# The last two row tiles of a graph layer: matrix products spread between transposes, row counts gathered, column sums copied by two engines

## The chip, the core and the metric

The kernel runs on one core of one Trainium2 chip. The metric is the device time of one execution in microseconds, the median of several runs. A core has five engines with instruction streams of their own: TensorE (matrix products and transposes, results in the accumulator memory PSUM), VectorE, ScalarE and GpSimd (element-wise work), and SyncE, which here only issues DMA transfers. Each works through its stream in order, and semaphores hold an instruction until what it needs is there.

## What is computed

Four graph layers run over 2708 nodes with 128 features each, on one dense 2708 x 2708 matrix `adj` in which few entries are not zero. Each layer normalises and rectifies its input, applies a graph operation, and adds the result to its input. The change concerns layer 0 and the start of layer 1.

```python
# layer 0
h = jnp.maximum(_layernorm(x, axis=-1), 0.0)
x = x + _L0_gnn_ref(h, adj)      # (adj.T @ h) / adj.sum(axis=0)[:, None]
# layer 1
h = jnp.maximum(_layernorm(x, axis=-1), 0.0)
x = x + _L1_gnn_ref(h, adj, ...) # messages gelu(s[i] + d[j] + b), weighted by adj[i, j], summed over j
# layer 2: aggregate adj @ h, then a gated recurrent unit
# layer 3: two heads of masked attention
```

Layer 1 needs one message for each entry of `adj` that is not zero. So layer 0, which reads all of `adj` anyway, also lists those entries.

## The kernel before

Rows are cut into 22 row tiles of 128 (the last has 20 rows) and the row tiles into six groups: five of four tiles and a last one of two (tiles 20 and 21, 148 rows in all). Columns are cut in two ways: for the products into six chunks (five of 512 columns and one of 148), for the lists into 22 blocks of 124.

Layer 0 does four things with each row tile:

- `load_row_tile` brings it from memory; two sets of four tiles are held at a time.
- `aggregate_rows(n, ci)` multiplies the normalised features of tile `n` with chunk `ci` of the tile, on TensorE, and adds to accumulator `ci`. Six accumulators of one PSUM bank each are filled over all 22 tiles: a tile has six such products.
- `turn_blocks(gi, j)`, called a turn below, transposes column block `j` of all tiles of group `gi` on TensorE into one of two PSUM buffers. ScalarE copies it out as `aT` and sums the columns by the way (`sums`), and a DMA writes it to memory for layers 2 and 3. A turn of the last group holds only two transposes and 148 columns.
- `list_row_tile` finds the entries: for each of the 22 blocks VectorE takes the eight largest values of every row (`val`) and their columns (`col`). `sign_sums` has ScalarE count a row's entries with one long pass over the tile and then copy the diagonal block `dg`, which GpSimd prepares.

The instructions are in an order written out by hand (`tc.manual_schedule()`). The loop over groups emits, for each of the 22 turns `j`, the turn, then the products that are due, and at turns 1, 3, 6, 8 and so on the lists and sign sums. For groups of four, products are spread over the turns, `len(steps) * (j + 1) // NT` of them by turn `j`. The first group is different: its products come ahead of all its turns (`ahead`). So it is with the last group too.

After the loop ScalarE copies the six accumulators from PSUM to `sumT` in on-chip memory, and VectorE turns the column sums into reciprocals (`deg`, `inv`). Layer 1 then takes over the same PSUM banks and much of the same on-chip memory.

Layer 1 begins with a start-up list of steps. `spread_sums(g)` transposes a group of `sumT` on TensorE. `enter(g)` scales it by `inv` and adds it to `x` on VectorE, with the moments for the next normalisation; `rows(g)` normalises on ScalarE; `turn_rows(g)` transposes back. `count_rows(t)` counts, for row tile `t`, how many of the eight values of each block and row are above zero, with two VectorE instructions, into `rows_n[:, t, :]`. `rank(t)` sums these counts over the rows above with one product on TensorE, which VectorE copies out (`ends`). `select_rows`, `finish_rows`, `fetch` and `place` build from that the matrices that pick source and destination rows; `destinations` and `split_destinations` make the messages' second half. From row tile 4 on, the counts are made inside the periods of layer 1 that follow, one per row tile. Steps of one engine follow each other in the order of this list.

Of the kernel before, what the change touches and what calls it, by code (L numbers as in the profile page):

```python
# [21 lines left out]
BF16 = mybir.dt.bfloat16  # L22
AF = mybir.ActivationFunctionType
ALU = mybir.AluOpType
AX = mybir.AxisListType
# [5 lines left out]
P = 128  # L31
N = 2708
D = 128
NT = (N + P - 1) // P
# [10 lines left out]
NB = (N + JB - 1) // JB  # L45
S = 8
# [14 lines left out]
def listed_layers(ctx: ExitStack, tc: tile.TileContext, x, adj, w, out, flag):  # L61
    nc = tc.nc
# [100 lines left out]
    keep = lists.enter_context(tc.tile_pool(name="keep", bufs=1))  # L163
# [21 lines left out]
    ends4 = keep.tile([P, NB, R], BF16, name="ends4")  # L185
    rows_n = keep.tile([P, NT, NB], BF16, name="rows_n")
    ends = keep.tile([P, NT, NB], BF16, name="ends")
    later = keep.tile([P, NB, E], BF16, name="later")
    nc.gpsimd.memset(later, 0.0)
    xb = [keep.tile([P, NB, C], BF16, name=f"xb{q}") for q in range(2)]  # L190
# [13 lines left out]
    with tc.tile_pool(name="l0c", bufs=1) as fix:  # L204
# [29 lines left out]
        def normal_rows(g):  # L234
            t, k = GROUPS[g]
            scale_rows(tiles_of(h, t, k), tiles_of(xs, t, k), rstd[:, t - 4 :], shifts[:, t - 4 :], AF.Relu)

        with (
            tc.tile_pool(name="l0", bufs=2) as rows,
            tc.tile_pool(name="l0k", bufs=2) as pool,  # L240
            tc.tile_pool(name="l0t", bufs=8) as turned,
            tc.tile_pool(name="l0p", bufs=1, space=PSUM) as acc,
        ):
            accs = [acc.tile([P, CH], F32, name=f"acc{c}") for c in range(len(CHUNKS))]
            sets, marks = {}, {}

            def load_row_tile(n):
                gi, q, m = n // 4, n % 4, size(n)
                if q == 0:
                    sets[gi] = rows.tile([P, 4, N], F32, name="a")  # L250
                if m < P:
                    nc.gpsimd.memset(sets[gi][:, q, :], 0.0)
                nc.sync.dma_start(sets[gi][0:m, q, :], adj[n * P : n * P + m, :])

            def list_row_tile(n):

                m = size(n)
                a = sets[n // 4][:, n % 4, :]
                d0 = n * P
                b0 = d0 // JB  # L260
                b1 = (d0 + m - 1) // JB
                c0, c1 = b0 * JB, min((b1 + 1) * JB, N)
                near = pool.tile([P, 3 * JB], F32, name="near")
                nc.gpsimd.tensor_copy(near[:, 0 : c1 - c0], a[:, c0:c1])
                nc.gpsimd.tensor_tensor(
                    near[:, d0 - c0 : d0 - c0 + m], a[:, d0 : d0 + m], offdiag[:, 0:m], ALU.mult
                )
                marks[n] = pool.tile([P, P], F32, name="dg")
                nc.gpsimd.tensor_tensor(marks[n][:, 0:m], a[:, d0 : d0 + m], ident[:, 0:m], ALU.mult)

                def block(b):
                    if b0 <= b <= b1:
                        return near[:, b * JB - c0 : b * JB - c0 + width(b)]
                    return a[:, b * JB : b * JB + width(b)]

                blocks = [b for b in range(NB) if not b0 <= b <= b1] + list(range(b0, b1 + 1))
                if n >= LATER:
                    late_blocks.extend((n, b) for b in range(NB) if not b0 <= b <= b1)
                    blocks = range(b0, b1 + 1)
                for k in range(0, NB, 2):  # L280
                    for b in blocks[k : k + 2]:
                        nc.vector.max(val[:, n, b, :], block(b))  # L282
                    for b in blocks[k : k + 2]:
                        nc.vector.max_index(col[:, n, b, :], val[:, n, b, :], block(b))  # L284

            def sign_sums(n):
                m = size(n)
                sign = pool.tile([P, N], BF16, name="sign")
                nc.scalar.activation(sign, sets[n // 4][:, n % 4, :], AF.Sign, accum_out=total[:, n : n + 1])
                dg = marks.pop(n)[:, 0:m]  # L290
                nc.scalar.activation(dg, dg, AF.Copy, accum_out=own[:, n : n + 1])

            def aggregate_rows(n, ci):
                c, cw = CHUNKS[ci]
                m = size(n)
                nc.tensor.matmul(  # L296
                    accs[ci][:, 0:cw], h[0:m, n, :], sets[n // 4][0:m, n % 4, c : c + cw],
                    start=(n == 0), stop=(n == NT - 1),
                )

            def turn_blocks(gi, j):
                g0, gk = GROUPS[gi]
                i0, iw = span(g0, gk)
                k = size(j)
                p = bank("p_T")
                for q in range(gk):
                    m = size(g0 + q)
                    nc.tensor.transpose(  # L308
                        p[0:k, q * P : q * P + m], sets[gi][0:m, q, j * P : j * P + k], ident[0:m, 0:m]
                    )  # L310
                aT = turned.tile([P, CH], F32, name="aT")
                nc.scalar.activation(aT[0:k, 0:iw], p[0:k, 0:iw], AF.Copy, accum_out=sums[0:k, j, gi : gi + 1])  # L312
                nc.sync.dma_start(adjT[0:k, j, i0 : i0 + iw], aT[0:k, 0:iw])

            with tc.manual_schedule():
                for n in range(8):
                    load_row_tile(n)
                    if n == 1:
                        load_rest()
                for gi, (g0, gk) in enumerate(GROUPS):  # L320
                    steps = [(n, ci) for n in range(g0, g0 + gk) for ci in range(len(CHUNKS))]
                    ahead = gi == 0 or gk < 4
                    for n in range(g0, g0 + gk):
                        if ahead:
                            for ci in range(len(CHUNKS)):
                                aggregate_rows(n, ci)
                        if n < 2:
                            list_row_tile(n)
                            sign_sums(n)
                            (sum_rows, sum_squares)[n](pool)  # L330
                    done = 0
                    for j in range(NT):
                        turn_blocks(gi, j)
                        now = len(steps) * (j + 1) // NT
                        for step in steps[done:now]:
                            if not ahead:
                                aggregate_rows(*step)
                        done = now
                        n = g0 + j // 5
                        if j % 5 == 1 and j // 5 < gk and n > 1:  # L340
                            list_row_tile(n)
                        if j % 5 == 3 and j // 5 < gk and n > 1:
                            sign_sums(n)
                        if gi > 0 and j % 4 == 3 and j < 16 and g0 + 4 + j // 4 < NT:
                            load_row_tile(g0 + 4 + j // 4)
                        if j == NT - 2 and gi + 1 < len(GROUPS):
                            normal_rows(gi + 1)
                for ci, (c, cw) in enumerate(CHUNKS):
                    nc.scalar.copy(sumT[:, c : c + cw], accs[ci][:, 0:cw])


        deg = fix.tile([P, 3, NT], F32, name="deg")
# [36 lines left out]
    with (  # L389
# [429 lines left out]

        with tc.manual_schedule():  # L820
            for step, n in (
                (spread_sums, 0), (count_rows, 0), (spread_sums, 1), (rank, 0), (enter, 0),
                (select_rows, 0), (describe, 0), (enter, 1), (spread_sums, 2), (rows, 0), (turn_rows, 0),
                (count_rows, 1), (rows, 1), (count_rows, 2), (count_rows, 3), (destinations, 0), (turn_rows, 1),
                (finish_rows, 0), (fetch_both, 0), (rank, 1), (enter, 2), (spread_sums, 3), (select_rows, 1),
                (split_destinations, 0), (destinations, 1), (describe, 1), (rows, 2), (turn_rows, 2),
                (place, 0), (pass_on, 0), (sources, 0), (enter, 3), (spread_sums, 4), (split_destinations, 1),
                (destinations, 2), (rows, 3), (turn_rows, 3), (finish_rows, 1), (fetch_both, 1), (enter, 4),
                (spread_sums, 5), (columns, 0), (place, 1), (split_destinations, 2), (destinations, 3), (rows, 4),
                (turn_rows, 4), (enter, 5), (rank, 2), (select_rows, 2), (rows, 5), (turn_rows, 5), (describe, 2),  # L830
                (split_destinations, 3), (put_values, 0), (destinations, 4), (put_rest, 0), (finish_rows, 2),
            ):
                step(n)
# [865 lines left out]
```

## Time and profile before

| | |
|---|---|
| time, median of 3 runs | 1076.99 us (1075.41 to 1079.09) |
| profiled execution, span | 1076.2 us |
| TensorE matmul busy | 950.2 us (88%) |
| VectorE busy | 824.4 us (77%) |
| ScalarE busy | 516.5 us (48%) |
| mean granted TensorE clock | 0.934 of full speed |

Busy time is the time in which an engine worked on an instruction. The idle time ahead of an instruction is put down to the engine or transfer that released it last, after the arrow: `[3.16 <-ACT hT L349]` is 3.16 us of idle time that ended when ScalarE's instruction of line 349, which writes `hT`, was done. (`hT` is the trace's name for the memory of `sumT`, which layer 1 uses again.) In the trace PE is TensorE's products and transposes, PEld its weight loads, DVE VectorE, ACT ScalarE, POOL GpSimd, SP SyncE; L and a number is a line of the kernel. The granted clock is the share of full speed at which TensorE was let run. The chain of work that ended last says little here: it reaches back only to 1069.26 us. So the timelines of single engines have to be read.

### The profile page before, as it was taken

The numbers are of one execution on the slowest core, as the hardware profiler recorded it, in microseconds if no ns is written. First come the engines' busy times: TensorE is split into PE (matmuls) and PEld (weight loads), VectorE is DVE, ScalarE is ACT, GpSimd is POOL, SyncE is SP. The second block draws the span as 40 slices with busy tenths as digits, with TensorE's granted clock in tenths as the row PEclk, the third lists the DMA queues.
The fourth block names the chain that finished last, engine by engine and source line by source line (L and its number), as shares of the span: only waits on it lengthen the run. The fifth ranks groups of instructions, "written<-read, shape, count | busy, mean of one in ns | idle before, by whom it ended". The sixth has DMA issues, their size and how long they took to land. (4 is left out here: it accounts for less than half of the span.)

```text
span 1076.2 us, 21996 instructions
## 1 busy us (share of the span) xinstructions
PE 950.2 (88%) x7950; PEld 756.6 (70%) x7950; DVE 824.4 (77%) x2856; ACT 516.5 (48%) x1431; POOL 398.0 (37%) x476
## 2 busy tenths in 40 slices
PE   5798889854699999999999979999978999999993
PEld 2454455433599999899998934444578999999762
DVE  7999999658577888887878265666578977997673
ACT  7777778444666566666576522333321200320142
POOL 3311112013686556666765253434410300440132
PEclk9999999755799999999999979999989999999996
DMA  9888897221133333223222065666300000000000
GB/s 367 312 308 291 311 344 257 57 72 55 54 124 103 118 115 112 83 85 108 85 89 75 29 215 199 206 215 211 106 21 26 7 3 1 6 16 1 1 16 14
DMA packets 60625, 129.67 MB, mean 120 GB/s; under 512 B 11160, under 2 KB 23828, under 8 KB 57798
## 3 DMA queue, kind: packets, MB, share of 16 engines
q1 hardware_dynamic: 58690, 125.38, 33.7%
q10 hardware_dynamic: 1816, 2.80, 0.8%
q8 instruction: 64, 1.05, 0.4%
q14 instruction: 55, 0.45, 0.1%
HBM read 81.55 MB, written 30.87 MB: 104 GB/s over the span
## 5 line engine op out<-in xcount | busy, mean ns | idle before, releaser
L949 PE MATMUL att<-hv,wt 128*128 128x129 f32 (+2 forms) x1936 | 243.8, 283 | 8.8 <-DVE wt L917 8.8
L949 PEld LDWEIGHTS att<-hv,wt 128*128 128x128 f32 (+2 forms) x1936 | 224.7, 192 | 25.7 <-DVE wt L917 10.2
L917 DVE SCALAR_TENSOR_TENSOR wt<-row,lift,mask 128x1024 f32<-128x1024 f32 (+5 forms) x176 | 160.2, 939 | 35.1 <-PE att L949 35.1
L530 POOL TENSOR_SCALAR put<-mine,value 128x128 f32<-128x128 bf16 x176 | 149.6, 866 | 70.3 <-DVE mine L427 68.0
L606 PE MATMUL p_m<-s,sel 128*128 128x128 bf16 x1452 | 161.6, 220 | 5.4 <-ACT g L618 5.4
L610 PE MATMUL p_m<-d,cols 124*128 124x128 bf16 (+1 forms) x1452 | 161.8, 220 | 1.4 <-DVE cols L560 1.3
L121 POOL TENSOR_TENSOR n_r<-n_r,minus_half 128x4 f32<-128x4 f32 (+1 forms) x31 | 46.1, 1486 | 292.4 <-DVE n_r L120 286.8
L631 PE MATMUL agg<-put,g 128*128 128x128 f32 (+1 forms) x968 | 135.9, 281 | 0.0
L296 PE MATMUL acc<-a,hs 128*128 128x512 f32 (+2 forms) x264 | 119.8, 563 | 11.1 <-ACT hs L137 11.1
L308 PEld LDWEIGHTS p_T<-ident,a 128*128 128x128 f32 x484 | 61.3, 147 | 85.7 <-issue 38.4
L631 PEld LDWEIGHTS agg<-put,g 128*128 128x128 f32 x968 | 118.2, 192 | 0.0
L1088 PE MATMUL p_agg<-a,hs 128*128 128x512 f32 (+2 forms) x264 | 109.4, 557 | 7.5 <-DMA a<-adjT 7.5
L606 PEld LDWEIGHTS <-sel 128*128 128x128 bf16 x1452 | 104.3, 98 | 10.8 <-issue 7.0
L308 PE MATMUL p_T<-ident,a 128*128 128x128 f32 x484 | 84.3, 295 | 30.9 <-ACT aT L312 23.5
L284 DVE FIND_INDEX8 col<-val,a 128x8 uint16<-128x124 f32 (+1 forms) x400 | 109.2, 290 | 0.0
L610 PEld LDWEIGHTS <-cols 124*128 124x128 bf16 (+1 forms) x1452 | 102.6, 98 | 1.9 <-DVE cols L560 1.9
L618 ACT ACTIVATE g<-p_m 128x512 f32<-128x512 f32 x132 | 73.0, 553 | 63.5 <-PE p_m L610 63.5
L538 ACT ACTIVATE put<-mine,value 128x128 f32<-128x128 bf16 x308 | 100.5, 391 | 0.0
L312 ACT ACTIVATE aT<-p_T 128x512 f32<-128x512 f32 (+2 forms) x132 | 71.1, 541 | 52.8 <-ACT aT L312 27.6
L282 DVE MAX8 val<-a 128x8 f32<-128x124 f32 (+1 forms) x400 | 94.2, 282 | 2.1 <-DMA a<-in_adj 2.1
L1088 PEld LDWEIGHTS p_agg<-a,hs 128*128 128x128 f32 (+1 forms) x264 | 47.6, 194 | 55.9 <-issue 54.3
L296 PEld LDWEIGHTS acc<-a,hs 128*128 128x128 f32 (+1 forms) x264 | 44.6, 199 | 31.2 <-issue 19.9
(249 smaller groups left out, 1423.7 us busy)
## 6 DMA issues: line engine op xcount, KB each, us to landing
a<-in_adj SPq DMA_DIRECT2D x21, 1354.0 KB
adjT<-aT SPq DMA_DIRECT2D x105, 256.0 KB
a<-adjT SPq DMA_DIRECT2D x20, 1280.0 KB
spread<-passed SPq DMA_DIRECT2D x22, 704.0 KB
later<-sel SPq DMA_DIRECT2D x22, 616.0 KB
row<-own_d ACTq DMA_DIRECT2D x10, 256.0 KB
later<-sel SPq DMA_DIRECT2D x22, 82.5 KB
adjT<-aT SPq DMA_DIRECT2D x21, 74.0 KB
```

The lines of the kernel that those rows point to most:

```text
L282: nc.vector.max(val[:, n, b, :], block(b))
L284: nc.vector.max_index(col[:, n, b, :], val[:, n, b, :], block(b))
L296: nc.tensor.matmul(accs[ci][:, 0:cw], h[0:m, n, :], sets[n // 4][0:m, n % 4, c : c + cw], start=(n == 0), stop=(n == NT - 1),)
L308: nc.tensor.transpose(p[0:k, q * P : q * P + m], sets[gi][0:m, q, j * P : j * P + k], ident[0:m, 0:m])
L530: nc.gpsimd.tensor_scalar(st["put", 0][:, b, :], st["mine"][:, b, :], st["value"][:, b : b + 1], None, ALU.mult)
L538: nc.scalar.activation(st["put", 1][:, b - HP, :], st["mine"][:, b, :], AF.Identity, scale=st["value"][:, b : b + 1])
L606: nc.tensor.matmul(p[:, b - b0, :], st["sel"][:, b, :], s3[:, q, t % 2, :], start=(q == 0), stop=False)
L610: nc.tensor.matmul(p[:, b - b0, :], st["cols"][0:kb, b, :], d3[0:kb, b, q, :], start=False, stop=(q == 2))
L631: nc.tensor.matmul(agg, g[:, b - 4 * k, :], put, start=(b == 0), stop=False)
L917: nc.vector.scalar_tensor_tensor(wt[0:kj, :], row[0:kj, k, c : c + n], lift[0:kj, j, k : k + 1], mask[0:kj, j, c : c + n], op0=ALU.max, op ...
L949: nc.tensor.matmul(banks[s // 3][0:m, s % 3, :], wt[0:kj, q * P : q * P + m], hv[0:kj, j, k, :], start=(v < 2 and s // 3 not in touched), ...
L1088: nc.tensor.matmul(pa[:, 0:n], h[0:k, j, :], a[0:k, j - j0, 0:n], start=(j == 0), stop=(j == NT - 1))
```

## The change

Three edits, all at the end of layer 0 and the start of layer 1.

First, the last group is no longer one whose products come ahead. One product follows each of its first twelve turns. Second, the counts of row tiles 0 to 3 are no longer four steps of layer 1's start-up. They are made at the end of layer 0 by two instructions over all four tiles at once, into a buffer of their own, `some4`, that is kept beside `rows_n`. Third, the copies of accumulators 0, 2 and 4 go to VectorE, and those of 1, 3 and 5 stay on ScalarE.

The aim of the first is to give ScalarE turns to copy while TensorE multiplies; of the second, to take small instructions out of the start-up; of the third, to have two engines share the copies that layer 1 waits for.

```diff
+    some4 = keep.tile([P, 4, NB, S], BF16, name="some4")
...
-                    ahead = gi == 0 or gk < 4
+                    ahead = gi == 0
...
-                        now = len(steps) * (j + 1) // NT
+                        now = len(steps) * (j + 1) // NT if gk == 4 else min(len(steps), j + 1)
...
+                nc.vector.tensor_scalar(some4, val[:, 0:4, :, :], 0.0, None, ALU.is_gt)
+                with nc.allow_low_precision("counts up to 8"):
+                    nc.vector.reduce_sum(rows_n[:, 0:4, :], some4, AX.X)
                 for ci, (c, cw) in enumerate(CHUNKS):
-                    nc.scalar.copy(sumT[:, c : c + cw], accs[ci][:, 0:cw])
+                    copy = nc.vector.tensor_copy if ci % 2 == 0 else nc.scalar.copy
+                    copy(sumT[:, c : c + cw], accs[ci][:, 0:cw])
...
-                (spread_sums, 0), (count_rows, 0), (spread_sums, 1), (rank, 0), (enter, 0),
+                (spread_sums, 0), (spread_sums, 1), (rank, 0), (enter, 0),
                 (select_rows, 0), (describe, 0), (enter, 1), (spread_sums, 2), (rows, 0), (turn_rows, 0),
-                (count_rows, 1), (rows, 1), (count_rows, 2), (count_rows, 3), (destinations, 0), (turn_rows, 1),
+                (rows, 1), (destinations, 0), (turn_rows, 1),
```

## The prediction

> **What bounds the kernel now.** I read the page first for the shares (TensorE busy 88%, VectorE 77%, ScalarE 48%). These are averages over four layers; the change touches only the last group of layer 0 and the hand-over to layer 1. I went from the page to the busy time by stretches, then to the timeline of each engine between 186 and 250 us. Columns of the stretches: length, busy time and count of TensorE matmuls, its weight loads, VectorE, ScalarE and GpSimd, then granted TensorE clock, DMA share, GB/s.
>
> ```profile
> 175.00:200.00 25.00, 23.22 (x90) 12.50 (x91) 25.00 (x171) 14.16 (x36) 3.65 (x9) 0.99 0.42 143
> 200.00:225.00 25.00, 17.12 (x57) 9.93 (x55) 7.45 (x49) 15.80 (x58) 0.68 (x3) 0.50 0.27 80
> ```
>
> Up to about 205 us VectorE is never idle (row lists) and sets the pace of layer 0. After that no engine is full: from 200 to 225 us VectorE works 7.45 us of 25. The timelines tell who waits for whom (start, length, engine, line, operation, count, idle time before it and its releaser):
>
> ```profile
> 190.03 11.37 PE L296 MATMUL acc<-a,hs 128*128 128x512 f32 x28
> 201.33 3.83 PE L308 MATMUL p_T<-ident,a 128*128 128x128 f32 x12
> ...
> 212.81 6.78 PE L308 MATMUL p_T<-ident,a 128*128 128x128 f32 x22 [2.18 <-ACT aT L312]
> 222.75 1.97 PE L758 MATMUL p_m<-ident,hT 128*128 128x128 f32 x8 [3.16 <-ACT hT L349]
> ```
>
> ```profile
> 202.11 0.29 ACT L312 ACTIVATE aT<-p_T 128x148 f32<-128x148 f32 x1 [10.68 <-issue]
> ...
> 209.74 2.45 ACT L289 ACTIVATE sign<-a 128x2708 bf16<-128x2708 f32 x1
> ...
> 220.06 2.64 ACT L349 COPY hT<-acc 128x512 f32<-128x512 f32 x6
> ```
>
> ```profile
> 219.80 0.25 DVE L421 TENSOR_SCALAR some<-val 128x176 bf16<-128x176 f32 x1 [14.32 <-ACT aT L312]
> ```
>
> The tail is a chain: TensorE does all 12 products of the two last row tiles (to 201.4 us) while ScalarE sits idle 10.68 us; then 22 turns go from TensorE to ScalarE and back, with two sign sums between them, to 220.15 us; then ScalarE copies six accumulators, and only then does TensorE start layer 1 at 222.75 us, 3.16 us idle. VectorE has nothing for 14.3 us.
>
> [...] the granted clock falls at 199.64, rises at 240.60 and falls at 244.01, and 40.96 is 12 times 3.41. The fall comes with TensorE full, in a window holding only products of the last tile, which has 20 rows:
>
> ```profile
> 192.81:196.23 3.42, 3.42 (x10) 1.00 0.00 0
> 196.23:199.64 3.41, 3.41 (x9) 1.00 0.00 0
> 199.64:203.05 3.41, 3.41 (x10) 0.50 0.01 2
> ```
>
> (TensorE alone: length, busy time and count, clock, DMA share, GB/s.) [...]
>
> **The change part by part.**
>
> *Products between the transposes.* Warm, the 512-column products of the last tiles follow each other every 0.86 us (two records 0.43 apart), the 148-column one takes about 0.25; at half clock double. A turn is two transposes: 0.30 us warm (four took 0.60), 0.63 cold. ScalarE needs 0.48 per turn (0.29 + 0.19) and 3.1 per row tile for sign sum and diagonal (2.45 + 0.19 + 0.30 + 0.19). Two PSUM buffers let TensorE run two turns ahead.
> New timeline from 191.2 us, where TensorE ends group 4: turns 0 to 3, each with a product, 1.16 apart; ScalarE ends turn 3 at 195.5. The sign sum of tile 20 keeps it to 198.6, so TensorE stalls before turn 6, from 197.5 to 199.0. Turns 6 to 8 with products of tile 21 follow warm to 202.5. The sign sum of tile 21 starts at 202.2 and the diagonal copy behind it needs GpSimd's tile: that product waits on VectorE's list and ends at 204.92 in before; VectorE's order there is unchanged. So ScalarE resumes at about 205.4. By then I expect the clock to have fallen (203.05, as the 20-row products again hold little work), so product 21/4 ends at 206.3 and turn 11 near 206.9. A short product (0.5), then ten cold turns at 0.63 and the last ScalarE pass end at about 214.3, against 220.15: **5.85 us**.
> Bounds: warm to the end, 13 turns at 0.48 after 205.4 end at 211.9 (8.2 us gained). Cold already from 199.64, the products take 1.72 each, tile 21's sign sum ends at 207.1 and the last turn at 217.2 (3.0 gained).
>
> *Copies on two engines.* Six copies took 2.64 us. ScalarE keeps two long and the short one: 2.64 - 3 x 0.47 = 1.2 us after the last turn. VectorE's three, about 0.68 each (a 128x387 evacuation took 0.555 and a 128x129 one 0.292, so 1.02 ns per element and 125 elements more), wait only for products that end by 207 and lie in its idle stretch. Gain **1.4 us**, since TensorE's first work of layer 1 waits for all copies to release the banks.
>
> *Counts in one go.* Two instructions over four tiles, scaled from 0.24 and 0.34 us for one tile: 0.8 to 1.4 each, in VectorE's idle 14 us after 205.4, ahead of the copies. Together with the three copies VectorE is done near 210, before the column sums that need the last turn. Eight small instructions leave the start of layer 1: four pairs of about 0.57. The first pair lay beside ScalarE's copies. The others lie before a wait that VectorE has anyway:
>
> ```profile
> 236.27 1.61 DVE L477 TENSOR_TENSOR sel<-sel,later 128x2816 bf16<-128x2816 bf16 x1
> ...
> 240.49 0.18 DVE L456 CAST ends<-p_r 128x22 bf16<-128x22 f32 x1 [2.61 <-PE p_r L455]
> ```
>
> There TensorE is held by its own order (transposes, ScalarE's copy, destination products, second transposes), so the 1.7 us removed only lengthen the 2.61 us wait. I count **0** (at most 1.7).
>
> *New waits.* VectorE's copy of the first accumulator waits for product 21/0; behind it queue the other copies and the column-sum chain, which cannot start before the last ScalarE pass anyway. TensorE's turns of the last group now wait behind products: the loss is in the timeline above.
>
> Sum: 5.85 + 1.4 = 7.2 us. Everything after the start of layer 1 is tied to it, not to absolute times; I see no transfer or earlier work that would pin a later stage. 1077.0 - 7.2 is **1069.8 us**, which I call 1070.0.
>
> **The rivals.**
> A, the clock falls early: [...] For it: windows with 0.76 and 1.14 us of busy time dropped the clock at 46.0 and 90.4 us. Against it: one with 1.77 us kept it, and I expect about 1.9. Gain 3.0 + 1.4: 1072.6.
> B, the tail shortens but layer 1's start gives it back, because VectorE or a weight load is late: the message weights are issued at 221.74 us only after the column-sum chain, which keeps its distance of 1.6 us from the last turn while the copies shrink by 1.4. Against it: their first user comes at 225.38, and destinations at 236.83. Only the copies would be left: 1075.6.
> C, slower: all the tail runs cold. 10 x 1.72 + 2 x 0.5 + 22 x 0.63 from 191.2 give a last turn near 223.4, 3.2 later; less 1.4, plus one more cold window when layer 1's dense products start (1.7 us): 1080.5. For it: 41 us after 199.64 are at half clock. Against it: the window before holds full 128-row products.
>
> **How the numbers follow.** Forecast 0.66 (gain 4.6 to 9.6), A 0.18, B 0.11, C 0.05. The bound warm case reaches 8.2 + 1.4, so 1067.4, the cold one 1072.6; with runs of before spread 1075.41 to 1079.09 I take about 1.5 us more at each end: 1066.0 to 1074.0, leaving out B, C and little else. Faster by over 0.3% (3.2 us) is the forecast and most of A, 0.84; within 0.3% is B and a part of A, 0.11; slower 0.05.
>
> **What would show it.** In the changed profile: ScalarE's idle gap of 10.68 us gone; the last turn at 212 to 217 us; three ScalarE copies of about 1.2 us together after it and three VectorE copies before it; layer 1's first transposes 6 to 9 us earlier; the wait before the second rank longer than 2.61 us. It would be wrong if the last turn comes after 218 us, if the distance from layer 1's first transposes to the dense products (284.97 us, where the clock rises) grows, or if the clock falls before 199 us.

## The result and the profile after

The changed kernel takes 1071.51 us (median of 4 runs, 1071.37 to 1073.93) where the kernel before, run beside it, takes 1077.44 (1075.41 to 1079.09). The ratio is 0.9951 with a 95% interval of 0.9929 to 0.9974, so the change saves about 5.9 us. A later series gave 0.9953 (0.9938 to 0.9969). The two profiled executions differ by 6.6 us (1076.2 and 1069.6).

The same stretches as before, of the kernel after (length, then TensorE, weight loads, VectorE, ScalarE, GpSimd, clock, DMA share, GB/s):

```profile
175.00:200.00 25.00, 23.23 (x97) 12.21 (x95) 25.00 (x171) 18.71 (x52) 3.37 (x8) 1.00 0.48 158
200.00:225.00 25.00, 17.79 (x53) 8.79 (x52) 15.89 (x71) 9.76 (x38) 3.71 (x6) 0.56 0.25 73
```

ScalarE's work moved forward: 18.71 us in the first stretch where it had 14.16. VectorE works 15.89 us in the second, where it had 7.45: its copies and counts lie in the idle stretch, and layer 1's start has moved in.

TensorE's timeline of the kernel after (start, length, line, operation, count, idle time before it and its releaser):

```profile
189.37 1.28 PE L297 MATMUL acc<-a,hs 128*128 128x512 f32 x4
190.49 0.44 PE L309 MATMUL p_T<-ident,a 128*128 128x128 f32 x2
190.85 1.12 PE L297 MATMUL acc<-a,hs 128*128 128x512 f32 x2
191.82 0.44 PE L309 MATMUL p_T<-ident,a 128*128 128x128 f32 x2
...
198.44 0.49 PE L309 MATMUL p_T<-ident,a 128*128 128x128 f32 x2 [0.42 <-ACT aT L313]
...
204.72 0.70 PE L309 MATMUL p_T<-ident,a 128*128 128x128 f32 x2
205.25 2.05 PE L297 MATMUL acc<-a,hs 20*128 20x512 f32 x2
207.23 0.70 PE L309 MATMUL p_T<-ident,a 128*128 128x128 f32 x2
207.77 0.84 PE L297 MATMUL acc<-a,hs 20*128 20x148 f32 x2
208.53 6.16 PE L309 MATMUL p_T<-ident,a 128*128 128x128 f32 x20
216.42 1.97 PE L764 MATMUL p_m<-ident,hT 128*128 128x128 f32 x8 [1.73 <-ACT hT L355]
```

Products and turns alternate from 190.49 us, and TensorE waits only 0.42 us for ScalarE's first sign sum. The starts tell the price: at full clock (warm, 1.00 granted) a turn and its product take 1.33 us (190.49 to 191.82), at half clock (cold, 0.50) 2.51 (204.72 to 207.23), of which the product takes 1.98. The wait before layer 1's first transposes fell from 3.16 to 1.73 us.

ScalarE and VectorE of the kernel after:

```profile
214.89 0.27 ACT L313 ACTIVATE aT<-p_T 20x148 f32<-20x148 f32 x1
215.06 0.18 ACT L313 ACTIVATION_READ_ACCUMULATOR aT<-p_T 20x1 f32 x1
215.16 1.21 ACT L355 COPY hT<-acc 128x512 f32<-128x512 f32 x3
```

```profile
205.03 0.51 DVE L350 TENSOR_SCALAR some<-val 128x704 bf16<-128x704 f32 x1
205.57 0.89 DVE L352 TENSOR_REDUCE rows_n<-some 128x88 bf16<-128x704 bf16 x1
206.38 1.88 DVE L355 COPY hT<-acc 128x512 f32<-128x512 f32 x3
215.28 0.29 DVE L360 TENSOR_REDUCE deg<-sums 128x22 f32<-128x132 f32 x1 [7.03 <-ACT aT L313]
```

Three ScalarE copies of 1.21 us follow the last turn; VectorE's counts and copies are done by 208.26 us and it then sits idle 7.03 us.

The clock (TensorE alone: length, busy time and count, clock, DMA share, GB/s):

```profile
199.67:203.08 3.41, 3.41 (x12) 1.00 0.25 73
203.08:206.49 3.41, 3.41 (x6) 0.50 0.17 45
```

It falls at about 203.08 us, after a stretch of 20-row products and turns in which TensorE was full (3.41 us of 3.41).

To compare runs I use four marks of each profiled execution: A, the start of group 4's last products (190.03 before, 189.37 after); T, the end of ScalarE's last turn; S, layer 1's first transposes; G, layer 1's first product of the gather (`agg<-put,g`). Times from A take out the up to 3 us by which executions differ on the way to the last group (A lies between 187.17 and 190.03 us). The table's distances are worked out from the timelines; "fall" is the clock's fall counted from A.

| kernel | fall | A to T | T to S | S to G | A to G | end |
|---|---|---|---|---|---|---|
| before | 9.6 | 30.12 | 2.60 | 66.8 | 99.5 | 1076.2 |
| after | 13.7 | 25.87 | 1.18 | 66.6 | 93.7 | 1069.6 |
| after, again | 12.3 | 27.07 | 1.17 | 66.7 | 94.9 | 1069.1 |
| products only | 12.6 | 26.69 | 2.61 | 66.7 | 96.1 | 1070.0 |
| copies only | 9.8 | 29.91 | 1.18 | 66.7 | 97.7 | 1071.0 |
| counts only | 8.2 | 31.51 | 2.60 | 66.8 | 100.9 | 1075.5 |
| all copies on VectorE | 12.5 | 29.79 | (-7.20) | 73.0 | 95.6 | 1069.4 |
| five copies on VectorE | 12.8 | 26.52 | 0.22 | 66.6 | 93.3 | 1067.1 |
| last tile over 128 rows | 20.5 | 24.66 | 1.18 | 66.6 | 92.5 | 1067.7 |
| alternating tiles | 16.9 | 26.11 | 1.17 | 66.6 | 93.9 | 1065.1 |
| five copies, 128 rows | 20.2 | 25.09 | 0.22 | 66.6 | 91.9 | 1067.1 |
| the same, late diagonal | 21.2 | 23.95 | 0.23 | 66.6 | 90.8 | 1064.0 |

In the last row the clock had also fallen 0.7 us after A and risen again at 4.1.

From G on, executions differ by up to 4 us in layers 2 and 3 (from layer 3's first product to the end 287.6 to 291.9 us), with no order by edit. I did not study this; it is why single spans are not compared here.

### The profile page after: what moved, and what is told of

Same layout as the page of the kernel before. It is cut to its first block, busy times and chain, and to the rows that moved or that the text cites. A ratio compares the mean times of both kernels' runs of the same rounds, so it can differ in the third digit from the quotient of the medians.

```text
span 1069.6 us, 21992 instructions
## 1 busy us (share of the span) xinstructions
PE 950.0 (89%) x7950; PEld 754.1 (71%) x7950; DVE 824.4 (77%) x2853; ACT 515.4 (48%) x1428; POOL 398.7 (37%) x476
## 5 line engine op out<-in xcount | busy, mean ns | idle before, releaser
L297 PE MATMUL acc<-a,hs 128*128 128x512 f32 (+2 forms) x264 | 124.4, 574 | 10.8 <-ACT hs L137 10.8
L297 PEld LDWEIGHTS acc<-a,hs 128*128 128x128 f32 (+1 forms) x264 | 44.7, 202 | 25.9 <-issue 14.8
```

The source lines that it names most:

```text
L297: nc.tensor.matmul(accs[ci][:, 0:cw], h[0:m, n, :], sets[n // 4][0:m, n % 4, c : c + cw], start=(n == 0), stop=(n == NT - 1),)
```

## The experiments

### Each part alone

The first leaves counts and copies as before:

```diff
-                    ahead = gi == 0 or gk < 4
+                    ahead = gi == 0
...
-                        now = len(steps) * (j + 1) // NT
+                        now = len(steps) * (j + 1) // NT if gk == 4 else min(len(steps), j + 1)
```

> Only the products of the last two row tiles are put between the turns; counts and copies stay as in the kernel before. Theory (the tail from the last group's start to the last turn shrinks by 4.2 us, the copies give 1.4 apart from it, the counts nothing): time 1073.2, the last ScalarE pass of the turns about 25.9 us after the start of group 4's last products (30.1 before), then 2.6 us until layer 1's first transposes as before. Rival (the counts or copies carry most of the gain): time above 1075.5, and less than 2 us shorter from group 4's last products to the last turn.

Measured: 1074.02 us, ratio 0.9970 (0.9952 to 0.9987). A to T is 26.69 us, T to S 2.61. The first rival falls: the products carry most of the gain. The 25.9 expected was missed by 0.8, and the clock had fallen 1.1 us earlier than in the kernel after.

The second shares the copies only:

```diff
-                    nc.scalar.copy(sumT[:, c : c + cw], accs[ci][:, 0:cw])
+                    copy = nc.vector.tensor_copy if ci % 2 == 0 else nc.scalar.copy
+                    copy(sumT[:, c : c + cw], accs[ci][:, 0:cw])
```

> Only the six copies are shared by VectorE and ScalarE. Theory: layer 1's first transposes start 1.2 us instead of 2.6 us after the last turn, the last turn stays 30.1 us after group 4's last products, time 1076.0. Rival (the copies lie beside other work, since the column-sum chain and weight loads hold layer 1 anyway): the first transposes come earlier but the distance from them to the end grows by the same 1.4 us, time 1077.4.

Measured: 1075.59 us, ratio 0.9992 (0.9978 to 1.0006), too near to no change for the time alone to decide. The trace decides: T to S is 1.18 us where it was 2.60, and S to G is 66.7, no longer than before (66.8). So 1.4 us is gained and not given back by G.

The third gathers the counts only:

```diff
+                nc.vector.tensor_scalar(some4, val[:, 0:4, :, :], 0.0, None, ALU.is_gt)
+                with nc.allow_low_precision("counts up to 8"):
+                    nc.vector.reduce_sum(rows_n[:, 0:4, :], some4, AX.X)
...
-                (spread_sums, 0), (count_rows, 0), (spread_sums, 1), (rank, 0), (enter, 0),
+                (spread_sums, 0), (spread_sums, 1), (rank, 0), (enter, 0),
...
-                (count_rows, 1), (rows, 1), (count_rows, 2), (count_rows, 3), (destinations, 0), (turn_rows, 1),
+                (rows, 1), (destinations, 0), (turn_rows, 1),
```

> Only the counts of row tiles 0 to 3 are gathered at the end of layer 0. Theory: nothing on the path, time 1077.4 within noise, the wait before VectorE's second rank copy grows from 2.6 to about 3.9 us. Rival (small VectorE instructions at layer 1's start are on the path): 1.0 to 1.7 us less between layer 1's first transposes and the end.

Measured: 1077.08 us, ratio 1.0000 (0.9987 to 1.0013). S to G is 66.8 us, as before. VectorE's timeline of this run shows where the removed time went:

```profile
233.74 1.62 DVE L481 TENSOR_TENSOR sel<-sel,later 128x2816 bf16<-128x2816 bf16 x1
239.23 0.18 DVE L460 CAST ends<-p_r 128x22 bf16<-128x22 f32 x1 [3.87 <-PE p_r L459]
```

The wait for TensorE's second rank is 3.87 us, where it was 2.61. The counts bought nothing in time. A to T is 1.4 us longer here than before; that is the clock, which fell 8.2 us after A, 1.4 us earlier than before, in the middle of the products (12.75 us of busy time, 11.37 before).

Added up, the medians of the three runs give 3.4 us (2.7 and 1.1, less 0.4), where the whole change gave 5.9 and later 4.7. Each of the three is uncertain by 1.4 to 1.9 us, so the times alone do not show that the parts add up, and no run joins just two of them. The traces do add up to G: the products alone take 96.1 us from A to G, less 1.4 for the copies 94.7, and the changed kernel takes 93.7 and 94.9.

### Are ScalarE's copies still on the path?

```diff
-                    copy = nc.vector.tensor_copy if ci % 2 == 0 else nc.scalar.copy
+                    copy = nc.vector.tensor_copy
```

> The changed kernel with all six copies on VectorE. Theory (ScalarE's three copies after the last turn still sit on the path, VectorE is idle 7 us before the column sums): VectorE's six copies take 3.8 us and end near 211, layer 1's first transposes start 0.1 to 0.2 us after the last turn, 1.0 to 1.1 us gained on the changed kernel: 1070.4. Rival (the column-sum chain of 1.3 us that starts after the last turn takes the place of the copies): the first transposes come 1.1 us earlier, but VectorE's first use of the reciprocals does not, time as the changed kernel, 1071.5.

Measured: 1071.66 us, ratio 0.9948 (0.9930 to 0.9966). It is as fast as the changed kernel, as the rival said, but for neither reason. The order between the two hand-written parts is not fixed: with no ScalarE copy behind the last turn, layer 1's transposes were placed among the turns. TensorE's timeline of this run:

```profile
210.10 0.69 PE L764 MATMUL p_m<-ident,hT 128*128 128x128 f32 x2 [1.13 <-DVE hT L355]
210.58 0.64 PE L309 MATMUL p_T<-ident,a 128*128 128x128 f32 x2
211.16 0.47 PE L764 MATMUL p_m<-ident,hT 128*128 128x128 f32 x1
211.43 0.64 PE L309 MATMUL p_T<-ident,a 128*128 128x128 f32 x2
```

TensorE waits 1.13 us for the last copy in the middle of the turns and then does other work between them. A to T grows to 29.79 us, and everything after needs the reciprocals that come only after T. So I kept the short copy on ScalarE, which holds the order:

```diff
-                    copy = nc.vector.tensor_copy if ci % 2 == 0 else nc.scalar.copy
+                    copy = nc.vector.tensor_copy if ci < 5 else nc.scalar.copy
```

> The changed kernel with five copies on VectorE and only the short one (148 columns) on ScalarE, so that TensorE's first transposes of layer 1 still stand after the last turn in its order. Theory: layer 1's first transposes start 0.3 us after the last turn (1.18 in the changed kernel), and 0.9 us less from group 4's last products to the end; time about 1070.6. Rival (the column-sum chain of 1.3 us after the last turn takes over): the first transposes start at 0.3 us, but the distance from them to the end grows by about as much, time as the changed kernel.

Measured: 1068.99 us, ratio 0.9932 (0.9908 to 0.9955). T to S is 0.22 us and S to G 66.6, so 1.0 us is gained from T to G and the column-sum chain does not take over. The theory holds, by the trace. By the medians this version is 2.5 us below the changed kernel, which was timed in another series; the intervals of the two ratios overlap, and the 1.5 us more are not explained.

### Why does the clock fall?

One run does the last tile's products over all 128 rows (the rows beyond 20 are zeros):

```diff
-                    accs[ci][:, 0:cw], h[0:m, n, :], sets[n // 4][0:m, n % 4, c : c + cw],
+                    accs[ci][:, 0:cw], h[:, n, :], sets[n // 4][:, n % 4, c : c + cw],
```

> The changed kernel with the products of the last tile over all 128 rows (the 108 rows beyond the 20 are zeros in both operands). Theory (the clock falls because 20-row products count as little work): the granted clock stays full until at least 207 us, products of the last tile stay at 0.97 us, the last turn ends 1.5 to 3.5 us earlier relative to group 4's last products (22.4 to 24.4 us after them, 25.9 in the changed kernel), time 1069. Rival (the clock falls for the idle gaps at the sign sums, or the zeros count as no work): the clock falls 12 to 15 us after group 4's last products as in the changed kernel, and nothing moves.

Measured: 1069.52 us, ratio 0.9929 (0.9907 to 0.9951). The last tile's 512-column products stand in the same place and take about as long (1.12 us of busy time each, 1.10 in the kernel after, both warm), and the clock holds longer (TensorE alone, columns as above):

```profile
197.82:201.23 3.41, 3.41 (x12) 1.00 0.27 77
201.23:204.65 3.42, 2.30 (x6) 1.00 0.07 19
204.65:208.06 3.41, 2.56 (x13) 1.00 0.29 85
208.06:211.47 3.41, 3.41 (x11) 0.50 0.43 126
```

It falls at 208.06 us, 20.5 after A, when the products are over and only turns are left. The stretch from 201.23 has more idle time (1.12 us) than the one after which the clock fell in the changed kernel (none), and the clock stays at 1.00 behind it. So in these two runs the fall goes with the rows of the products (20 rows, 13.7 us after A; 128 rows, 20.5), not with TensorE's idle time. The other runs agree: all three with 128 rows keep the clock to 20.2 to 21.2 us after A (one of them after a short early fall, see below), the five that spread 20-row products one tile after the other lose it at 12.3 to 13.7. (There are falls after idle time too: in the kernel after the clock also fell at 158.72 us, after a stretch in which TensorE was busy 1.38 us of 3.41.) A to T is 24.66 us, 1.2 less than after. That is less than the 1.5 to 3.5 expected, because another wait now ends last. ScalarE's and TensorE's timelines of this run:

```profile
204.67 0.22 ACT L292 ACTIVATE dg<-dg 128x20 f32<-128x20 f32 x1 [1.94 <-POOL dg L270]
```

```profile
205.30 0.49 PE L309 MATMUL p_T<-ident,a 128*128 128x128 f32 x2 [1.78 <-ACT aT L313]
```

ScalarE stands at tile 21's diagonal copy for 1.94 us, and TensorE behind it for 1.78. In the second profile of the changed kernel ScalarE stood there too, for 2.25 us, but TensorE, at half clock, was still busy with products and did not wait. With the clock held it is done with them earlier and has to wait.

The other run lets the two tiles alternate:

```diff
+                    if gk < 4:
+                        steps.sort(key=lambda s: s[1])
```

> The changed kernel with the products of tiles 20 and 21 taking turns (20/0, 21/0, 20/1, 21/1 ...). Theory (20-row products count as little work): [...] the clock holds about 3.4 us longer, to 206 us or later, and the last turn ends 0.5 to 2 us earlier; time 1070.5. Rival: the clock falls where it did, nothing moves.

Measured: 1067.83 us, ratio 0.9921 (0.9893 to 0.9949). The clock holds to 204.22 us, 16.9 after A, 3.2 longer than after, as the theory said. But A to T is 26.11 us, no shorter: ScalarE waits 2.17 us at the same diagonal copy, and TensorE 2.57 behind it. So this fall came after idle time as well: TensorE was busy 2.00 us in the stretch ahead of it. The low time of this run arises mostly in layer 3 (287.6 us to the end, 288.9 to 291.9 in the others), where no edit reaches, so I don't credit it to the order of the tiles.

### Both, and the wait behind them

Five copies on VectorE together with 128 rows:

> Both: five copies on VectorE and the last tile's products over 128 rows. If both theories hold, the last turn ends 22.4 to 24.4 us after group 4's last products, layer 1's first transposes 0.3 us later, time about 1068. If only the first holds, 1070.6.

Measured: 1068.30 us, ratio 0.9934 (0.9909 to 0.9958). T to S is 0.22 us as expected, A to T 25.09, which misses the 22.4 to 24.4 for the wait just named (2.33 us of ScalarE here). The last run moves that diagonal copy:

```diff
-                dg = marks.pop(n)[:, 0:m]
+                if n < NT - 1:
+                    own_sums(n)
+
+            def own_sums(n):
+                dg = marks.pop(n)[:, 0 : size(n)]
                 nc.scalar.activation(dg, dg, AF.Copy, accum_out=own[:, n : n + 1])
...
+                        if gi == len(GROUPS) - 1 and j == 16:
+                            own_sums(NT - 1)
```

> Five copies on VectorE, the last tile's products over 128 rows, and ScalarE's diagonal copy of tile 21 moved from behind its sign sum (turn 8) to behind turn 16, with its own wait on GpSimd. Theory (with the clock held, the next bound of the tail is ScalarE waiting at that copy for GpSimd's block, which waits for VectorE's list: 1.94 us idle until 204.67 in the run before): that wait is gone, the last turn ends 1.5 to 2.5 us earlier, 22.5 to 23.5 us after group 4's last products, and layer 1's first transposes 0.2 us later; time about 1066.5. Rival (TensorE or VectorE ends the tail anyway): the last turn stays at 24.7 to 25.1 us, time about 1068.3.

Measured: 1066.55 us, ratio to before 0.9916 (0.9894 to 0.9939); the changed kernel in the same series took 1071.62. The wait is gone; ScalarE's timeline of this run:

```profile
203.79 0.28 ACT L317 ACTIVATE aT<-p_T 128x148 f32<-128x148 f32 x1
...
208.09 0.21 ACT L296 ACTIVATE dg<-dg 128x20 f32<-128x20 f32 x1
```

It takes up the turns at 203.79 us, straight after the sign sum. A to T is 23.95 us, outside the 22.5 to 23.5 expected. The clock had fallen at 187.88 us, 0.7 after A and before the last group's first turn (188.66), and rose at 191.30, so the group's first product was cold: 2.08 us of busy time, against 1.12 for the later, warm ones. ScalarE's first sign sum starts 7.50 us after A, 5.91 in the kernel after; by this estimate the cold start cost 1.6 us of the tail. This version beats the changed kernel: 5.1 us by the medians of this series, 4.1 us up to G (90.8 against 94.9 from A).

The changed kernel itself, run beside it:

> The changed kernel once more, beside the next one. Every theory: about 1071.5. From its trace: if the clock falls in another place relative to the last group, the distance from group 4's last products to the last turn moves with it (25.9 us when it fell 13.7 us after them, 26.5 to 26.7 when it fell 12.6 to 12.8 us after them); from layer 1's first transposes to its first gather product 66.7 us as in all runs.

Measured: 1071.62 us, ratio 0.9953 (0.9938 to 0.9969). The clock fell 12.3 us after A and A to T was 27.07 us: earlier fall, longer tail, as expected.

## Why the prediction was right

- **What bounds the tail.** Right. With the products spread alone, A to T fell by 3.4 us (30.12 to 26.69), and ScalarE's idle gap of 10.68 us is gone.
- **Products between the transposes, 5.85 us.** Right in kind, too large: 4.25 in the profiled pair (30.12 less 25.87). The term that was off is the price of a turn and its product: I took 1.16 us warm and 2.35 cold (0.63 + 1.72), and they take 1.33 and 2.51; the short cold product I took at 0.5 takes 0.76. Up to the first sign sum this cost nothing: TensorE comes to it later, but then waits 0.42 us instead of 1.5 and goes on only 0.1 us later than predicted (all relative to A). After that the third product of tile 21 ends 0.7 us later, the fifth 1.6, the last turn 1.6.
- **Why the pair was dearer.** That the kinds take turns is not the reason. In group 4 of the kernel before they do so already, with four transposes to a product:

```profile
184.85 0.60 PE L308 MATMUL p_T<-ident,a 128*128 128x128 f32 x4
185.29 1.02 PE L296 MATMUL acc<-a,hs 128*128 128x512 f32 x2
186.15 0.60 PE L308 MATMUL p_T<-ident,a 128*128 128x128 f32 x4
```

By the starts this pair takes 0.44 + 0.86 = 1.30 us. With two of the four transposes it should take less, but in the kernel after it takes 0.36 + 0.97. What is new is the second transpose of each turn, which is over 20 rows. In group 4 a transpose starts 0.11 us after the one ahead of it. In the kernel after the 20-row one starts 0.20 us after the 128-row one, the product 0.16 after that, and the product's second half 0.53 later instead of 0.43. My estimate from these distances is that the time goes where the number of rows changes; no run tests this.
- **The clock.** Predicted to fall at 203.05 us, 13.0 after A. It fell at 203.08, which is 13.7 after A, and in the second profile at 199.55, 12.3 after A. That the first agrees to 0.03 us is luck, since A moves by up to 3 us between executions. The reason given, 20-row products, is the one that the 128-row run supports (fall 20.5 us after A). Rival A, a fall one stretch earlier for the wait at the first sign sum, did not come: that wait is 0.42 us. But where the fall lands moves the tail: T comes 25.87 us after A in the first profile and 27.07 in the second, so the 4.25 above holds for one pair of profiles only. Three profiles without spread products have 29.91 to 31.51, four with them (the changed kernel twice, products only, five copies) 25.87 to 27.07.
- **GpSimd's block at the diagonal copy.** Predicted to hold ScalarE until 205.4, 15.4 us after A. In the kernel after ScalarE takes up turns at 204.81, also 15.4 after A, but its sign sum had just ended, so GpSimd did not hold it. In the second profile it did. TensorE was at half clock both times and did not wait for it; with the clock held it did.
- **Copies, 1.4 us.** T to S fell from 2.60 to 1.18: 1.42. Alone the same. The copies of the two engines never run at the same time here: VectorE's are done at 208.26 us, ScalarE's begin at 215.16. Elsewhere both engines read PSUM at the same time: in the run with the late diagonal VectorE's five copies (206.42 to 209.49 us) run beside ScalarE's copies of turns. They take 3.07 us, as long as five of 0.68 us started 0.60 apart would at the pace of the kernel after (4 x 0.60 + 0.68 = 3.08), and a turn's copy takes 0.29 us in both.
- **Counts, 0.** S to G is 66.8 before and 66.8 with the counts alone. Two instructions took 0.51 and 0.89 us in idle time, and the wait before the second rank is 3.87 us in the kernel after, longer than 2.61, as predicted.
- **Rivals B and C.** S to G did not grow, so nothing was given back; the tail did not run cold from its start.
- **The warm bound.** Its sum is slightly off: 13 turns of 0.48 us from 205.4 end at 211.6, not 211.9.

Sum: 4.25 + 1.42 is 5.7 of the 7.2 predicted, near the 5.9 of the medians. The remaining 0.9 between the two profiles is an arrival at A 0.66 us earlier and 0.27 after S, neither of which I put down to the change.

## What to carry to other kernels

When two engines hand work to and fro and one has independent work in a block ahead of that, spread it between the hand-overs: it fills waits that both engines have (ScalarE's idle gap of 10.68 us is gone here), up to the point where one of them is full (here TensorE from 199.67 us, 3.41 us of 3.41). Price such a mix from a stretch in which the same shapes follow each other in the same order: no warm stretch of the kernel before had a 20-row transpose next to a product, and the prices read there were too low. Small instructions are worth removing only where no wait follows them on the same engine; read that wait first (here it grew from 2.61 to 3.87 us). And when a bound falls, look for the next instruction that stands in order behind something late: here moving one diagonal copy shortened A to T by 1.1 us (25.09 to 23.95), and the counts gave nothing.

## What the runs showed of the hardware

- Products over 20 rows took about as long as over 128 (1.10 and 1.12 us of busy time, warm), but the clock fell among them, at 203.08 us in the kernel after, with TensorE full in the stretch ahead (3.41 us of 3.41). With 108 rows added to them it held 6.8 us longer (20.5 against 13.7 us after A), although these rows are zeros.
- TensorE's busy time alone does not tell when the clock falls: in the 128-row run it fell at 208.06 us, after a stretch busy 2.56 us of 3.41 with turns and one short product, while the stretch ahead of it, busy 2.30 with mostly long products, kept it. One of the two transposes of each turn is over 20 rows, so the runs do not tell whether the fall at 208.06 us goes with these rows or with the transposes themselves.
- VectorE's copies of accumulators of 512 columns took 0.68 us each in the kernel after, as estimated, and started 0.60 us apart (three in 1.88). Five took 3.07 in the run with the late diagonal, with ScalarE's passes over turns beside them, 0.29 us each.
